# Feeding the second batch beside its own attention, and loading the base by whole parities on GpSimd's queue

## The chip, the cores and the metric

One core of one Trainium2 chip runs the whole kernel. The metric is the device time of one launch in microseconds (us). The engines are called PE (TensorE, matrix products and transposes), DVE (VectorE), ACT (ScalarE), POOL (GpSimd) and SP (SyncE, which only issues transfers here). SP, ACT and POOL each issue DMA transfers in the order of their own instruction queue; a transfer that has to wait for a semaphore makes that queue wait.

## What is computed

Two layers on an input of 2 batches, 128 channels and 64 x 64 positions (L = 4096 tokens of 128 channels per batch). Cut to what matters:

```python
# layer 0: group norm, q/k/v with rotary positions, 4 heads of softmax attention, projection
x = xi + w_proj @ attention(q, k, v) + b_proj
# layer 1, on tokens t of shape (2, 4096, 128)
t = t + softmax(ln(t) @ ln(t).T) @ ln(t)
u = ln(t)
# u convolved along the tokens with 16 spectral filters (plus and minus),
# each result mixed by a 128 x 128 matrix; and three taps of the tokens themselves
t = t + sum_k conv(u, phi_k) @ M_k + sum_i shift(u, i) @ M_u[i]
```

`ln` is a layer norm over the 128 channels. A choice among four branches (by `log_weights + gumbel`) scales the matrices and masks the tail of the sequence.

## The kernel before, in words

The program is written with a tile framework: a tile has a tag and a number of buffers, the framework sets all semaphores, and its scheduler places instructions on the queues near the order of the program; `ordered` and `keep_in_program_order` pin an instruction to that order. Side work is written as Python generators: the main loop calls `next(beside)` at fixed places, and each call emits one step of the side work between the main loop's instructions.

**Stages.** `layer0` runs both batches' first layer. `attend16(0, ...)` is layer 1's attention of batch 0, `attend16(1, ...)` that of batch 1. Then the filter stage: four quarters, one for each batch `b` and parity `ro` of the token blocks, of eight chunks with two steps each, 64 steps in all. Last comes the output.

**Attention (`attend16`, L1241).** The 4096 tokens are eight rows `j` of 512. The 36 pairs (j, i) with i >= j are taken row by row; a turn n handles the scores of pair n (twelve products `y`, L1252), exponentials on ACT (L1261), a 16-bit high part (L1265) and rest (L1266), the direct product `od` of pair n-1, and the transposed product `oa` of pair n-2 (both L1280), whose operand `eT` is made by DMA transposes on SP's queue (L1271). DVE adds up denominators from `eT` (`both`, L1300) and the products (L1292, L1312). A row is finished by `close(j)` (L1314 on), which updates `tok[b]` and calls `closed(j)`: for batch 1 this takes the row's layer norm statistics (`fed`, with the power on POOL, L108), and loads and splits two mixing matrices (L1517 to L1519). `next(beside)` is called four times in a full turn. At the end a loop runs what is left of `beside`.

**Feed (`feed`, L1364).** For a batch it turns the finished tokens into what the filter stage reads. Row `i` of eight: four normalised blocks `un` (L743 through `stats.normed`); for both halves of a transform a product `pf` (L1403), split on ACT and DVE into `uh` (L1375, L1376) and written to DRAM, `rows16[b]`, by four transfers (L1409, L1410); a transpose `uT` (L1422, L1423); the taps, that is a transpose `tT` of the tokens (L1382), three products `ar` (L1387), a sum `oc` (L1390) and its write to DRAM, `base[b]` (L1391). Each of these is a step ended by `yield`. `un`, `uh` and `oc` have two buffers. The taps of row 0 come last, since they need the last row. Feed 0 writes on POOL's queue (`aside`), feed 1 on SP's. Feed 0 runs beside attention 1, with buffers in that stage's pool, and is followed there by the loads of the first step's tables and tokens (`fetch16(0, 4)`, one piece in three calls). Feed 1 runs beside the first quarter of the filter stage, after four empty calls, with buffers in the pool `late`.

**Filter stage.** A step loads 2 MB of tables on SP's queue and 512 KB of tokens (from `rows16[b]`) on POOL's, each for two steps later and into the third of three buffers (`fetch16`, L1202 on; the tokens are L1213, the tables L1222). `convolve16` makes sixteen products `cv` (L1591), ACT and DVE split them into a high part and a rest (L1598, L1599), and `mix16` of the step before adds 48 products `m` (L1607) to an accumulator that is copied out once per chunk to `oh` (L1614). Between four parts of each step, `next(beside)` is called once.

**Back (`back`).** Beside the following quarter, `oh` of a parity is turned (transposes `vt`, L1709, copies L1710) and taken through the inverse transform (`bk`, L1719) in four blocks `p4`; DVE adds the base of the block (`had`, L1721). Outside the last parity a block's base is one transfer of 256 KB on SP's queue into a single buffer (L1703), asked for when the block's turn comes; the first block comes after five empty calls. The last parity has its own loads at the end.

Of the kernel before, what the change touches and what calls it, by code (L numbers as in the profile page):

```python
# [12 lines left out]
F32 = mybir.dt.float32  # L13
# [9 lines left out]
P = 128  # L23
# [22 lines left out]
WC = 4  # L46
# [30 lines left out]
def conv_attn_hybrid(ctx: ExitStack, tc: tile.TileContext, io):  # L77
# [39 lines left out]
    def chain(*parts):  # L117
        for p in parts:
            yield from p
# [638 lines left out]
    def layers(st, layer0, in_halves):  # L758
# [479 lines left out]
        def halves16(n):  # L1238
            return list(zip(tables_in[n % 3], tokens_in[n % 3]))

        def attend16(b, p, beside, closed):  # L1241

            den = p.tile([P, NT, NQ], F32, tag="den", name=f"den{b}")
            oT = p.tile([P, NQ, 512], F32, tag="oT", name=f"oT{b}")
# [113 lines left out]
                        whole = j  # L1358
                    next(beside, None)
            close(whole)  # L1360
            for _ in beside:
                pass

        def feed(b, p, bank, fw, stats=None):  # L1364

            queue = aside if b == 0 else nc.sync


            if stats is None:
# [8 lines left out]
            def taps(i, uT):  # L1378
                oc = p.tile([P, 4, P], F32, tag="oc", name=f"oc{b}_{i}", bufs=2 if in_halves else 1)
                pt = bank(f"tT{b}_{i}").rearrange("p (t c) -> p t c", c=C)  # L1380
                for t in range(4):
                    nc.tensor.transpose(pt[:, t, :], tok[b][:, 4 * i + t, :], ident)  # L1382
                nc.scalar.copy(oc, pt)
                yield
                pa = bank(f"ar{b}_{i}").rearrange("p (t c) -> p t c", c=C)
                for n in range(NU):
                    nc.tensor.matmul(pa, mu[:, n, :], uT[:, 2 - n : 6 - n, :], start=(n == 0), stop=(n == NU - 1))  # L1387
                    if n == 0:
                        yield
                nc.vector.tensor_tensor(oc, pa, oc, ALU.add)  # L1390
                queue.dma_start(base[b][:, 4 * i : 4 * i + 4, :], oc)  # L1391
                yield

            before = first = None
            for i in range(NQ):
                un = p.tile([P, 4, C], F32, tag="un", name=f"un{b}_{i}")
                for t in range(4):
                    stats.normed(un[:, t, :], 4 * i + t)
                yield
                for c in range(2):  # L1400
                    at = BP + 1 + 2 * i
                    pf = bank(f"pf{b}_{i}_{c}").rearrange("p (t c) -> p t c", c=C)
                    nc.tensor.matmul(pf, fw[:, c, :], un, start=True, stop=True)  # L1403
                    if in_halves:
                        uh = p.tile([P, 2, 4, C], F16, tag="uh", name=f"uh{b}_{i}_{c}")
                        uhr = uh.rearrange("w h (p r) d -> w h p r d", r=2)
                        parts(uh, pf)
                        for h in range(2):
                            queue.dma_start(to[:, c, h, 2 * i : 2 * i + 2, :], uhr[:, h, :, 0, :])  # L1409
                            queue.dma_start(to[:, c, h, at : at + 2, :], uhr[:, h, :, 1, :])  # L1410
                    else:
                        uh = p.tile([P, 4, C], F32, tag="uh", name=f"uh{b}_{i}_{c}")
                        uhr = uh.rearrange("w (p r) d -> w p r d", r=2)
                        nc.scalar.copy(uh, pf)
                        queue.dma_start(to[:, c, 2 * i : 2 * i + 2, :], uhr[:, :, 0, :])
                        queue.dma_start(to[:, c, at : at + 2, :], uhr[:, :, 1, :])
                    yield

                uT = p.tile([P, 6, P], F32, tag="uT0" if i == 0 else "uT", name=f"uT{b}_{i}", bufs=1 if i == 0 else 2)
                pt = bank(f"uT{b}_{i}").rearrange("p (t c) -> p t c", c=C)  # L1420
                for t in range(4):
                    nc.tensor.transpose(pt[:, t, :], un[:, t, :], ident)  # L1422
                nc.vector.tensor_tensor(uT[:, 2:, :], pt, mask.unsqueeze(1).to_broadcast([P, 4, P]), ALU.mult)  # L1423
                if i:
                    nc.vector.tensor_copy(uT[:, :2, :], before[:, 4:, :])
                    yield
                    yield from taps(i, uT)
                else:
                    first = uT
                    yield  # L1430
                before = uT
# [25 lines left out]
        with ExitStack() as l1:  # L1457
# [3 lines left out]
            with ExitStack() as part:  # L1461
# [13 lines left out]
                    second_parts(i + 1)  # L1475

                second_parts(0)
                fw = transform(p1)

                def closed(j):  # L1480
                    gate[0] = j + 1
# [15 lines left out]
            if in_halves:  # L1497
                early = pool(middle, "early", side="right")
                tables_early = [early.tile([P, BP, NS, 2 * NK], F16, name=f"tables_e{n}") for n in range(2)]
                tokens_in = [  # L1500
                    [early.tile([P, NS, C], F16, name=f"tokens{turn}_{n}") for n in range(2)] for turn in range(3)
                ]
                tables_in.append(tables_early)
            if in_halves:
                mxr, mxl = mixing
            else:
                mxr, mxl = (x[0].rearrange("p (k s c) -> p k s c", k=NK, s=2) for x in (hiT, loT))
            with ExitStack() as part:
                p = pool(part, "l1_b", 2)
                fed = LayerStats(ffw, tok[1], "f1")  # L1510

                def closed(j):
                    fed.take(range(4 * j, 4 * j + 4))
                    fed.close(range(4 * j, 4 * j + 4))
                    own = slice(2 * j, 2 * j + 2)
                    m = p.tile([P, 2, 2, C], F32, tag="m", name=f"m{j}")
                    aside.dma_start(m, mx[own].rearrange("k p s c -> p k s c"))  # L1517
                    nc.vector.tensor_copy(mxr[:, own], m)
                    nc.vector.tensor_tensor(mxl[:, own], m, mxr[:, own], ALU.subtract)  # L1519

                if in_halves:
                    attend16(1, p1, chain(feed(0, p, bank, fw), spaced(fetch16(0, 4))), closed)
                else:
                    attend(1, p1, feed(0, p, bank, fw), closed)
        psum_a.close()
# [1 line left out]

        pc = pool(st, "ff_psum", space=bass.MemoryType.PSUM)
        pf = pool(st, "ff_x")
        late_pool = pool(right1, "late", 2, side="right")  # L1530

        if in_halves:
            second = px.tile([P, 2, BP, NS, 2 * NK], F16, tag="a", name="tables_a")
# [139 lines left out]
        def back(b, ro, oh, outs, p):  # L1673
# [2 lines left out]
            ohr = oh.rearrange("e (w p c) -> e c p w", c=2, p=BP)  # L1676
            baser = base[b].rearrange("c (q r) j -> c r q j", r=2)
            if not end:
                for _ in range(WC + 1):
                    yield  # L1680
            if ro == 0:
# [14 lines left out]
            def turned(p4):  # L1696

                u = f"{b}_{ro}_{p4}"
                if end:
                    had, v = ends[p4][0], ends[p4][1].rearrange("p (c q) x -> p c q x", c=2)  # L1700
                else:
                    had = p.tile([P, 4, P], F32, tag="had", name=f"had{u}", bufs=1)
                    nc.sync.dma_start(had, baser[:, ro, 4 * p4 : 4 * p4 + 4, :])  # L1703
                    v = p.tile([P, 2, 4, C], F32, tag="v", name=f"v{u}", bufs=1)
                for c in range(2):
                    pt = pc.tile([P, 512], F32, tag="cv", name=f"vt{u}_{c}", bufs=3) if end else one_bank(f"vt{u}_{c}")
# [33 lines left out]

        outs = [None, None]
        late = iter(())
        fw = transform(late_pool)
        beside = chain([None] * WC, feed(1, late_pool, one_bank, fw, fed))
        steps = 0
        for b in range(B):
            for ro in range(2):
# [168 lines left out]
```

## Time and profile before

| what | us |
|---|---|
| median of 3 runs (lowest, highest) | 2737.7 (2715.2, 2753.86) |
| the profiled execution | 2752.7 |
| its span, first to last instruction | 2750.9 |
| PE busy in the span | 2580.7 (94%) |
| ACT busy | 1838.6 (67%) |
| DVE busy | 1671.5 (61%) |
| POOL busy | 437.6 (16%) |
| DMA share of the SP queue (q1), of 16 engines' span | 33.4% |
| DMA share of the POOL queue (q0) | 12.2% |

"Busy" doesn't count the issue of transfers or waiting. An average over the span hides the stages, which have different limits; so the working below reads stretches of 55 us, the waits inside a stage, and the order of issues on a queue. In a line of waits, "A <- B: total, times, longest" says that A's engine sat idle until B was done. In a timeline, the columns are start, length, engine, line and operation, with the idle time before it and what ended it in brackets. The trace records each 32-bit matrix product of PE as two.

### The profile page before, as it was taken

The numbers are of one execution on the slowest core, as the hardware profiler recorded it, in microseconds if no ns is written. First come the engines' busy times: TensorE is split into PE (matmuls) and PEld (weight loads), VectorE is DVE, ScalarE is ACT, GpSimd is POOL, SyncE is SP. The second block draws the span as 40 slices with busy tenths as digits, with TensorE's granted clock in tenths as the row PEclk, the third lists the DMA queues.
The fourth block names the chain that finished last, engine by engine and source line by source line (L and its number), as shares of the span: only waits on it lengthen the run. The fifth ranks groups of instructions, "written<-read, shape, count | busy, mean of one in ns | idle before, by whom it ended". The sixth has DMA issues, their size and how long they took to land.

```text
span 2750.9 us, 32560 instructions
## 1 busy us (share of the span) xinstructions
PE 2580.7 (94%) x11955; PEld 1276.4 (46%) x11955; DVE 1671.5 (61%) x2946; ACT 1838.6 (67%) x2059; POOL 437.6 (16%) x716
## 2 busy tenths in 40 slices
PE   5999999999998999999989996888989999899998
PEld 3555555555544454444444442433444444344444
DVE  5256564246367427888976776655556666566664
ACT  4999999999998897666545563444435554454553
POOL 2022121012122401000333101111111111111110
PEclk9999999999999999999999998999999999999999
DMA  5122220012113514766466955666656666665661
GB/s 145 35 66 66 64 70 20 5 53 66 30 34 98 80 42 83 123 110 105 98 136 124 162 106 132 140 152 154 164 163 175 206 195 156 171 202 176 186 185 59
DMA packets 350827, 311.92 MB, mean 113 GB/s; under 512 B 293296, under 2 KB 302144, under 8 KB 334464
## 3 DMA queue, kind: packets, MB, share of 16 engines
q1 hardware_dynamic: 295920, 231.18, 33.4%
q0 software_dynamic: 53296, 76.13, 12.2%
q10 hardware_dynamic: 1440, 2.43, 0.3%
q8 instruction: 96, 1.57, 0.2%
q14 instruction: 75, 0.61, 0.1%
HBM read 212.53 MB, written 23.33 MB: 86 GB/s over the span
## 4 chain that ended last, share of the span: by engine, by line
PE 63%; DMA 18%; DVE 10%; ACT 6%; issue 2%; SPq 0%; POOL 0%; DVEq 0%; ACTq 0%; POOLq 0%
PE m L1607 17%; PE acc L209 11%; PE s L209 11%; PE cv L1591 5%; DMA rows<-uh 5%; PE od L1280 5%; ACT e L465 5%; PE y L1252 5%; PE oa L1280 4%; DMA had<-base 4%; DMA eT<-pair 2%; DMA tables_b<-tables 2%; DMA tables_a<-tables 2%; DVE x L1599 1%; DVE pair L1266 1%
## 5 line engine op out<-in xcount | busy, mean ns | idle before, releaser
L465 ACT ACTIVATE e<-s 128x1536 f16<-128x1536 f32 (+1 forms) x704 | 938.7, 1425 | 57.0 <-PE s L209 52.3
L1598 ACT CAST x<-cv 128x1024 f16<-128x1024 f32 x512 | 493.6, 1016 | 411.6 <-PE cv L1591 402.5
L1599 DVE TENSOR_TENSOR x<-cv,x 128x1024 f16<-128x1024 f32 x512 | 602.5, 1219 | 267.9 <-ACT x L1598 267.9
L1607 PE MATMUL m<-x,mxr 128*128 128x512 f16 x2048 | 623.4, 381 | 0.0
L209 PE MATMUL acc<-e,v 128*97 128x512 f16 x2048 | 560.1, 381 | 16.3 <-DVE accs L413 13.7
L209 PE MATMUL s<-qs,ks 128*128 128x512 f16 x2048 | 560.5, 381 | 7.3 <-ACT e L465 3.8
L1607 PE MATMUL m<-x,mxl 128*128 128x512 f16 x1024 | 393.2, 384 | 3.2 <-DVE oh L1614 3.2
L209 PEld LDWEIGHTS <-v 128*97 128x97 bf16 x2048 | 255.8, 125 | 230.3 <-issue 29.8
L1261 ACT ACTIVATE ey<-y,nshift 128x512 f32<-128x512 f32 x288 | 196.1, 687 | 189.9 <-PE y L1252 161.7
L1607 PEld LDWEIGHTS <-mxr 128*128 128x128 f16 x2048 | 201.5, 98 | 243.6 <-issue 6.6
L209 PEld LDWEIGHTS <-ks 128*128 128x128 f16 x2048 | 201.2, 99 | 229.4 <-issue 46.9
L1213 POOL DMA_DIRECT2D tokens<-rows x256 | 155.9, 613 | 864.0 <-PE cv L1591 840.6
L1252 PE MATMUL y<-bothT 128*128 128x512 f16 x864 | 204.4, 382 | 3.3 <-ACT ey L1261 2.4
L1266 DVE TENSOR_TENSOR pair<-ey,pair 128x1024 f16<-128x1024 f32 x144 | 175.0, 1219 | 35.4 <-ACT pair L1265 34.8
L1280 PE MATMUL od<-pair,hi 128*128 128x512 f16 x576 | 184.6, 381 | 5.7 <-DVE oT L1292 4.6
L1300 DVE SCALAR_TENSOR_TENSOR both<-eT 128x512 f16<-128x512 f16 x224 | 153.7, 686 | 48.0 <-DMA eT<-pair 43.6
L413 DVE COPY accs<-acc 97x512 f32<-97x512 f32 x64 | 44.2, 690 | 211.0 <-PE acc L209 210.9
L1591 PEld LDWEIGHTS <-tokens 128*128 128x128 f16 x1024 | 101.3, 100 | 148.8 <-issue 50.2
L1607 PEld LDWEIGHTS <-mxl 128*128 128x128 f16 x1024 | 101.4, 99 | 133.7 <-DVE oh L1614 10.6
L1280 PEld LDWEIGHTS <-hi 128*128 128x128 f16 x1024 | 100.8, 98 | 122.3 <-issue 7.0
L1265 ACT CAST pair<-ey 128x1024 f16<-128x1024 f32 x144 | 150.7, 1047 | 6.5 <-DMA eT<-pair 3.3
L1280 PE MATMUL oa<-eT,hi 128*128 128x512 f16 x448 | 142.8, 380 | 0.9 <-DMA eT<-pair 0.9
(223 smaller groups left out, 2298.9 us busy)
## 6 DMA issues: line engine op xcount, KB each, us to landing
tables_a<-tables SPq DMA_DIRECT2D x42, 1024.0 KB
tables_b<-tables SPq DMA_DIRECT2D x42, 1024.0 KB
tables_e<-tables SPq DMA_DIRECT2D x42, 1024.0 KB
tokens<-rows POOLq DMA_DIRECT2D x256, 128.0 KB, 14.3
tab<-in_rot SPq DMA_DIRECT2D x32, 512.0 KB
ks<-term POOLq DMA_DIRECT2D x112, 64.0 KB, 2.2
qs<-term POOLq DMA_DIRECT2D x112, 64.0 KB, 2.0
accs<-back SPq DMA_DIRECT2D x32, 128.0 KB
```

Source lines behind the costliest of these rows:

```text
L209: tc.keep_in_program_order(nc.tensor.matmul(*args, **kw))
L465: nc.scalar.activation(e[:, own, :], ps[:, own, :], AF.Exp, scale=SCORE_SCALE)
L1213: nc.gpsimd.dma_start(ut[64 * copy : 64 * copy + 64], rows16[b].rearrange("h c r w d -> (h c) r w d")[:, row : row + BP, w0 : w0 + NS, :],)
L1252: nc.tensor.matmul(ps[:, q, :], a[0][:, bass.ts(t, P)], c[0][:, bass.ts(i, 512)], start=(n == 0), stop=(n == 2),)
L1261: nc.scalar.activation(e[:, q, :], ps[:, q, :], AF.Exp, bias=nshift16, accum_out=den[:, t, i : i + 1])
L1266: nc.vector.tensor_tensor(pair[:, 1, own], e, pair[:, 0, own], ALU.subtract)
L1280: nc.tensor.matmul(acc, a[0][:, own], pair(m, t), start=(start and t == 0 and n == 0), stop=(stop and t == 3 and n == 2),)
L1300: nc.vector.scalar_tensor_tensor(both, eT[:, 0, :, u, :], 1.0, eT[:, 1, :, u, :], ALU.mult, ALU.add, accum_out=den[:, 4 * i + u, j : j + 1],)
L1591: ordered(nc.tensor.matmul(pu[:, h, :], ut[:, at, :], tt[:, :, at, :], start=True, stop=True))
L1598: nc.scalar.copy(hi, pur)
L1599: nc.vector.tensor_tensor(lo, pur, hi, ALU.subtract)
L1607: nc.tensor.matmul(acc, m, x, start=(s == 0 and i == 0), stop=(s == 1 and i == len(products) - 1))
```

## The change

It has four parts.

1. `feed` of batch 1 moves from the filter stage into attention 1. It gets a `gate`: row `i` is fed only once `closed(i)` has been called, otherwise the call passes without work. It follows feed 0, taking turns (`by_turns`) with the loads of the first step. What has not been done when attention ends goes on beside the filter stage (`drain=False`), with PSUM buffers of that stage (`banked`), and without the four empty calls.
2. Both feeds use POOL's queue, the pool `late` (now opened before attention 1) and one copy of the transform `fw`, loaded after attention 0.
3. A tap has no pause any more between its first and its second product.
4. `back`, except for the last parity, loads the base of a whole parity in one transfer of 1 MB on POOL's queue, before its empty calls; the four blocks read slices of it.

```diff
--- before.py
+++ after.py
@@ -1238,7 +1238,7 @@
         def halves16(n):
             return list(zip(tables_in[n % 3], tokens_in[n % 3]))
 
-        def attend16(b, p, beside, closed):
+        def attend16(b, p, beside, closed, drain=True):
 
             den = p.tile([P, NT, NQ], F32, tag="den", name=f"den{b}")
             oT = p.tile([P, NQ, 512], F32, tag="oT", name=f"oT{b}")
@@ -1358,12 +1358,13 @@
                         whole = j
                     next(beside, None)
             close(whole)
-            for _ in beside:
-                pass
-
-        def feed(b, p, bank, fw, stats=None):
-
-            queue = aside if b == 0 else nc.sync
+            if drain:
+                for _ in beside:
+                    pass
+
+        def feed(b, p, bank, fw, stats=None, gate=None):
+
+            queue = aside
 
 
             if stats is None:
@@ -1385,7 +1386,7 @@
                 pa = bank(f"ar{b}_{i}").rearrange("p (t c) -> p t c", c=C)
                 for n in range(NU):
                     nc.tensor.matmul(pa, mu[:, n, :], uT[:, 2 - n : 6 - n, :], start=(n == 0), stop=(n == NU - 1))
-                    if n == 0:
+                    if n == 0 and not in_halves:
                         yield
                 nc.vector.tensor_tensor(oc, pa, oc, ALU.add)
                 queue.dma_start(base[b][:, 4 * i : 4 * i + 4, :], oc)
@@ -1393,6 +1394,8 @@
 
             before = first = None
             for i in range(NQ):
+                while gate is not None and gate[0] <= i:
+                    yield
                 un = p.tile([P, 4, C], F32, tag="un", name=f"un{b}_{i}")
                 for t in range(4):
                     stats.normed(un[:, t, :], 4 * i + t)
@@ -1475,7 +1478,7 @@
                     second_parts(i + 1)
 
                 second_parts(0)
-                fw = transform(p1)
+                fw = None if in_halves else transform(p1)
 
                 def closed(j):
                     gate[0] = j + 1
@@ -1501,6 +1504,10 @@
                     [early.tile([P, NS, C], F16, name=f"tokens{turn}_{n}") for n in range(2)] for turn in range(3)
                 ]
                 tables_in.append(tables_early)
+                late_pool = pool(right1, "late", 2, side="right")
+                fw = transform(late_pool)
+                banked = [bank]
+                fed_to = [0]
             if in_halves:
                 mxr, mxl = mixing
             else:
@@ -1517,9 +1524,16 @@
                     aside.dma_start(m, mx[own].rearrange("k p s c -> p k s c"))
                     nc.vector.tensor_copy(mxr[:, own], m)
                     nc.vector.tensor_tensor(mxl[:, own], m, mxr[:, own], ALU.subtract)
+                    if in_halves:
+                        fed_to[0] = j + 1
 
                 if in_halves:
-                    attend16(1, p1, chain(feed(0, p, bank, fw), spaced(fetch16(0, 4))), closed)
+                    ahead = spaced(fetch16(0, 4))
+                    feed_1 = feed(1, late_pool, lambda name: banked[0](name), fw, fed, fed_to)
+                    beside = chain(feed(0, late_pool, bank, fw), by_turns(ahead, feed_1))
+                    attend16(1, p1, beside, closed, drain=False)
+                    for _ in ahead:
+                        pass
                 else:
                     attend(1, p1, feed(0, p, bank, fw), closed)
         psum_a.close()
@@ -1527,7 +1541,8 @@
 
         pc = pool(st, "ff_psum", space=bass.MemoryType.PSUM)
         pf = pool(st, "ff_x")
-        late_pool = pool(right1, "late", 2, side="right")
+        if not in_halves:
+            late_pool = pool(right1, "late", 2, side="right")
 
         if in_halves:
             second = px.tile([P, 2, BP, NS, 2 * NK], F16, tag="a", name="tables_a")
@@ -1676,6 +1691,9 @@
             ohr = oh.rearrange("e (w p c) -> e c p w", c=2, p=BP)
             baser = base[b].rearrange("c (q r) j -> c r q j", r=2)
             if not end:
+                if in_halves:
+                    whole = p.tile([P, BP, P], F32, tag="had", name=f"had{b}_{ro}", bufs=1)
+                    aside.dma_start(whole, baser[:, ro])
                 for _ in range(WC + 1):
                     yield
             if ro == 0:
@@ -1699,8 +1717,11 @@
                 if end:
                     had, v = ends[p4][0], ends[p4][1].rearrange("p (c q) x -> p c q x", c=2)
                 else:
-                    had = p.tile([P, 4, P], F32, tag="had", name=f"had{u}", bufs=1)
-                    nc.sync.dma_start(had, baser[:, ro, 4 * p4 : 4 * p4 + 4, :])
+                    if in_halves:
+                        had = whole[:, 4 * p4 : 4 * p4 + 4, :]
+                    else:
+                        had = p.tile([P, 4, P], F32, tag="had", name=f"had{u}", bufs=1)
+                        nc.sync.dma_start(had, baser[:, ro, 4 * p4 : 4 * p4 + 4, :])
                     v = p.tile([P, 2, 4, C], F32, tag="v", name=f"v{u}", bufs=1)
                 for c in range(2):
                     pt = pc.tile([P, 512], F32, tag="cv", name=f"vt{u}_{c}", bufs=3) if end else one_bank(f"vt{u}_{c}")
@@ -1740,8 +1761,11 @@
 
         outs = [None, None]
         late = iter(())
-        fw = transform(late_pool)
-        beside = chain([None] * WC, feed(1, late_pool, one_bank, fw, fed))
+        if in_halves:
+            banked[0] = one_bank
+        else:
+            fw = transform(late_pool)
+            beside = chain([None] * WC, feed(1, late_pool, one_bank, fw, fed))
         steps = 0
         for b in range(B):
             for ro in range(2):
```

## The prediction, made before the changed kernel was run

> **What bounds the kernel now.** I read the table of fixed stretches first, because it shows stage by stage whether TensorE (PE) is full. Columns: stretch, length, busy time and count of PE, PEld, DVE, ACT, POOL, then PE clock, DMA share, GB/s.
>
> ```profile
> 1385.00:1440.00 55.00, 48.20 (x197) 22.56 (x196) 39.70 (x93) 24.42 (x50) 17.65 (x26) 0.94 0.69 136
> 1550.00:1605.00 55.00, 55.00 (x260) 25.49 (x259) 41.98 (x97) 36.65 (x78) 1.76 (x2) 1.00 0.69 127
> 1660.00:1715.00 55.00, 35.18 (x138) 14.74 (x138) 32.26 (x53) 22.71 (x25) 8.18 (x12) 0.83 0.60 135
> 1770.00:1825.00 55.00, 40.12 (x166) 17.72 (x164) 24.38 (x28) 17.83 (x21) 4.87 (x8) 0.89 0.65 148
> 1990.00:2045.00 55.00, 43.74 (x209) 22.38 (x208) 27.67 (x27) 20.74 (x23) 6.08 (x10) 0.88 0.55 174
> 2100.00:2155.00 55.00, 54.79 (x254) 24.67 (x253) 37.65 (x34) 31.32 (x33) 9.73 (x16) 1.00 0.61 203
> ```
>
> PE is full with attention alone (1550) and with the filter stage alone (2100). It has holes where the second batch's feed runs beside the filter stage (1660 to 1990), where the base is fetched (1990), and, smaller, where the first batch's feed runs beside attention (1385). The holes are the gain; work that PE does anyway only changes its place.
>
> To size them I used the timeline of the copies of finished accumulators (L1614), one per chunk; the eighth ends a quarter.
>
> ```profile
> 1994.03 0.59 ACT L1614 COPY oh<-m 128x512 f32<-128x512 f32 x1 [1.09 <-PE m L1607]
> ...
> 2242.53 0.59 ACT L1614 COPY oh<-m 128x512 f32<-128x512 f32 x1 [1.10 <-PE m L1607]
> ```
>
> The first convolution starts at 1658.25, so quarter 1 takes 335.8 us; the others (ends 2242.53, 2488.79, 2726.68) take 248.5, 246.3 and 237.9. Undisturbed chunks lie 27.8 apart (2159.19 to 2214.82 is two), so a bare quarter is 222.6.
>
> Next, who waits in quarter 1 (1657 to 2000), by total:
>
> ```profile
> ACT uh L1375 <- DMA rows<-uh: 60.9, 5, 19.6
> DVE uh L1376 <- ACT uh L1375: 54.0, 14, 18.7
> ...
> PE pf L1403 <- DVE uh L1376: 28.7, 3, 15.6
> ```
>
> ACT cannot refill a `uh` buffer before its write to DRAM is done; DVE waits for ACT, PE for DVE. The page's DMA part and SP's timeline say why the write is late:
>
> ```profile
> tokens<-rows POOLq DMA_DIRECT2D x256, 128.0 KB, 14.3
> ...
> rows<-uh POOLq DMA_DIRECT2D x64, 64.0 KB, 3.0
> ```
>
> ```profile
> 1683.21 10.48 SPq L1410 DMA_DIRECT2D rows<-uh  x1
> ...
> 1805.58 13.73 SPq L1222 DMA_DIRECT2D tables_e<-tables  x2
> ```
>
> The same 64 KB write lands in 3.0 us from POOL's queue in attention; on SP's it stands among 1 MB table loads, its issue alone takes 10 us, and the chain shows such writes at 21 to 37 us.
>
> Last, the chain of waits about 1985 to 2045:
>
> ```profile
> 1985.31 29.47 DMA had<-base
> ...
> 2015.93 23.15 DMA had<-base
> ```
>
> Two base loads in a row hold the end: same queue, one buffer, asked for about three calls before use.
>
> **What the Trainium skill says.** "DMA: Bandwidth & Descriptors", Queues, rings and completion order: each DMA engine consumes a queue's descriptors in ring order and alternates between queues by packets. The trace agrees: 3.0 us on POOL's queue against 21 to 37 behind tables. Same page, Anatomy of one DMA: a semaphore wait is spent on the issuing engine, so what stands behind it on that queue waits too; POOL spends 840.6 us so, in front of token loads. "TensorE: Matmul & The Clock Gate", HAM oscillation: idle gaps make the clock drop; the trace has 0.83, 0.89 and 0.88 in the three stretches with holes. So I cost holes by quarter lengths, which contain the slow clock, not by idle time.
>
> **The change, part by part.**
>
> *Feed's PE work.* Eight rows issue 32 pf and 48 ar records at 0.43 us spacing, 64 transposes at 0.11 and 4 pl: 13.8 + 20.7 + 7.0 + 0.4 = 42 us. Quarter 1 is then 222.6 + 42 + 13 (1658.25 to 1671.40, first convolution before the first mix) + **58 of stall**.
>
> *How much moves.* Attention of batch 1 makes 144 calls on its side work: two, later three or four, per block pair. With one pause fewer in each tap, feed 0 needs 59 and ends at the 16th of 36 pairs. Then table prefetch (24) and feed 1 alternate. Rows close at turns 10, 17, 23, 28, 32, 35 and 37 of 38, so the gate lets rows 0 to 4 and most of row 5 through: 33 of feed 1's 50 steps. Left for the filter stage are row 5's taps, rows 6 and 7, and the end: 2.6 + 5.2 + 5.2 + 3.4 = 16 us of PE. So 26 us of PE work moves: −26 in quarter 1, +26 in attention, nothing in sum.
>
> *Quarter 1.* All 64 row writes, 8 base writes and the ul pair leave SP's queue. On POOL's they come after the step's token loads, whose wait (for PE to release the buffer) ends when that step begins; 14.3 us landing of tokens is the nearest row for a write behind them, and a `uh` buffer is wanted again some 21 us later. I take 4 us of remaining stall (0 to 12). At the start, feed work lands in the fill, where DVE is the chain: 4 × 0.34 for un and 2 × 0.69 for uh, +3; but PE has over 9 us free there, which take 4 of the 16. Quarter 1: 222.6 + 13 + 3 + 16 − 4 + 4 = 255, **−81**.
>
> *Attention of batch 1.* +26 of PE. New stalls: in feed 0's phase (1334 to 1512) PE gaps add up to 13 us over eight rows, most of them pf waiting for un, which stands on DVE behind additions that wait for transposes:
>
> ```profile
> DVE both L1300 <- DMA eT<-pair: 34.6, 13, 7.1
> ...
> PE pf L1403 <- DVE un L743: 10.5, 5, 5.3
> ```
>
> That is 1.6 per row, 9 for 5.6 rows. DVE gets 4.4 us per row (un 4 × 0.34, uh 2 × 0.69, uT 0.98, oc 0.69), 25 in all, and has 13 of 55 free at 1550. A row taken as soon as it closes also waits for its statistics: POOL's power (1.2 us) comes between DVE's last statistic and un. Against that, alternating calls leave more time between un and pf. I take **+10** (−10 to 35: the lower end, since nothing excludes that feed fills gaps now empty, 7 of them after 1512). With the PE work **+36**.
>
> *Quarters 2 to 4.* Transposes and inverse cost PE 96 × 0.11, 11 us per parity. Stall: 248.5 − 222.6 − 11 = 15; 246.3 − 222.6 − 11 = 13; the last has a mix without convolution (24.2 for 27.8), 237.9 − 219 − 11 = 8. Twelve loads of 256 KB leave SP; three of 1 MB go to POOL, asked for at the first call of a quarter, needed at the eighth: 7 × 3.47 = 24 us. The trace has no such load. Lower end: 768 KB of the same 512-byte pieces took 9.2 us in a quiet place (mu_raw), 12 scaled (the skill's formula in Anatomy, 2.0 + bytes/436e3, would make it 4.4; the trace decides). Upper end: 512 KB of tokens lands in about 15, so 1 MB behind them 45. I take 25 to 28, since DMA is only 0.61 busy in this stage: 2 us of stall in each where there was one. In quarter 3 most of the stall isn't the base: its first two chunks (to 2311.69) exceed 55.6 by 13.6, the PE work and 3; 10 us appear after the output writes issued at 2304. Those stay. Savings: 13 + 3 − 2 + 6 = **−20**. Issue time on POOL (74 moved issues at 0.6 to 0.7, three at 1 to 1.5) is covered by its waiting; without that cover it would be 55 us of delay to tokens. The second fw load (256 KB) goes: nothing waited for it.
>
> **Sum.** −81 + 36 − 20 = −65 against the profiled 2752.7: 2688. That execution is 15 above the median of 2737.7. If the 15 are stalls that the change removes anyway, the result stays at 2688; if they lie elsewhere it is 2673. I take two thirds of the way: **2678**, −2.2%.
>
> **Rivals.**
> 1. *Attention pays more.* Transposes, table prefetch and row writes share the DMA engines just there: the stretch 1495 to 1550 has a share of 0.92 and a transpose of 9.6 us. Stalls at 35 instead of 10: 2703 (2698 to 2728). Against it: at 1550, with prefetch running, PE lacked nothing. Chance 0.17.
> 2. *The feed stays late* (scheduling puts it into the filter stage after all), or *the base stays late*. Quarter 1 is then 222.6 + 13 + 42 + 10 = 288, −48, and attention pays nothing: with the base −68, about 2675, so place hardly matters, the queue does. If the base stays late, 20 are lost: 2698. Together 0.10, half each.
> 3. *More is gained*: feed 1 fills idle PE in attention, and output writes meet a less loaded queue: 20 better, 2658. Chance 0.15.
> 4. *Slower: tokens behind the base load.* If 1 MB takes 31 us on POOL's queue, at the rate of tokens, the next step's tokens land at 14 + 31 + 15 = 60 us from the quarter's start; they are needed at three steps, 41.7. 18 of stall in three quarters, and the 20 not saved: 2678 + 54 + 20 = 2752, above the median before. It decides once that load takes over 13 us beyond tokens. For it: tokens already take up to 30.5 us. Against: 38% of DMA time is free here. 0.05.
>
> **Numbers.** The forecast has 0.53, own range 2660 to 2697. Its part below 2683 (2% below the median, about what a measurement of this kernel can tell from no change), some 0.6 of it, and rival 3 are faster, and the late feed of rival 2 about as often as not: 0.32 + 0.15 + 0.03 = 0.50. Slower by over 2% (above 2792) only if rival 4 is worse than priced or unseen: 0.03. The rest, 0.47, lies within. The range from 2645 to 2722 leaves out rival 4 and the tails of 1 and 3, about 0.2.
>
> **What would show it.** Right: SP issues only tables, transposes and outputs after 1310; ACT's wait for row writes under 10 us; quarter 1 at 250 to 262; attention's end 30 to 45 later; DVE's wait for had (37.7) under 8; gaps after the outputs remain. Wrong: od or pf gaps of 5 us in attention (rival 1), convolutions waiting for tokens in a quarter's first four steps (rival 4), or row writes still holding ACT in quarter 1.

## The result, and the profile after

| | median, us | lowest to highest | runs |
|---|---|---|---|
| before | 2736.03 | 2715.2 to 2759.44 | 20 |
| changed | 2717.82 | 2701.15 to 2758.58 | 20 |

The ratio is 0.9938 (95% interval 0.991 to 0.9966): faster, but by 0.6% where 2.2% was forecast. A second set of runs gave 0.9968 (0.9932 to 1.0003), and medians of 2741.49 against 2737.54 before, so that set shows no gain. Ratios leave out executions more than 1.5% above the fastest of their kernel; the first profile of the changed kernel (2752.85 us) and those of queue_deep and pause_pool are such executions, so no stage length is read from them, and the lines here are from a second profile of the changed kernel (after_again, 2712.15 us, span 2710.1).

The stretches of the second profile, with the columns of the prediction's first table; attention of batch 1 ends at 1709, quarter 1 at 1982:

```profile
1385.00:1440.00 55.00, 46.34 (x174) 21.18 (x172) 38.00 (x85) 22.72 (x48) 22.24 (x31) 0.88 0.58 122
1550.00:1605.00 55.00, 53.73 (x248) 25.15 (x247) 40.51 (x88) 34.33 (x73) 11.13 (x15) 1.00 0.78 146
1720.00:1775.00 55.00, 53.28 (x239) 25.15 (x238) 39.68 (x44) 28.07 (x34) 20.89 (x32) 1.00 0.64 205
1815.00:1870.00 55.00, 38.93 (x154) 16.04 (x153) 22.50 (x20) 19.00 (x20) 8.44 (x15) 0.81 0.55 141
1985.00:2040.00 55.00, 55.00 (x303) 31.71 (x302) 37.54 (x36) 26.54 (x30) 7.87 (x13) 1.00 0.59 178
2100.00:2155.00 55.00, 53.80 (x249) 24.13 (x248) 36.99 (x32) 30.05 (x32) 9.77 (x16) 1.00 0.59 200
```

The hole where the base was fetched is closed (1985), and PE is nearly full where the feed now ends beside the filter stage (1720). One new hole stands at 1815 with a clock of 0.81, after the feed is over. The copies that end quarters 1 and 2:

```profile
1982.54 0.58 ACT L1629 COPY oh<-m 128x512 f32<-128x512 f32 x1 [1.09 <-PE m L1622]
...
2216.55 0.58 ACT L1629 COPY oh<-m 128x512 f32<-128x512 f32 x1 [1.09 <-PE m L1622]
```

Stage lengths by such copies, in us, for all kernels below. Attention 1 runs from the last transposes of batch 0's attention to the first convolution.

| kernel | attention 1 | quarters 1 to 4 | ratio to before (95%) |
|---|---|---|---|
| before | 335.8 | 335.8, 248.5, 246.3, 237.9 | |
| after_again | 379.7 | 273.1, 234.0, 240.8, 229.4 | 0.9968 (0.9932 to 1.0003) |
| queue_only | 334.3 | 316.9, 248.8, 233.3, 232.6 | 0.9898 (0.986 to 0.9936) |
| move_only | 381.2 | 248.6, 233.3, 235.4, 239.1 | 0.9848 (0.9801 to 0.9895) |
| base_only | 334.2 | 332.1, 235.8, 244.8, 232.2 | 0.992 (0.9884 to 0.9956) |
| pinned | 382.9 | 250.2, 248.1, 233.5, 229.4 | 0.9936 (0.99 to 0.9973) |
| base_act | 383.0 | 258.6, 256.7, 251.6, 259.6 | 1.0095 (1.0059 to 1.0131) |
| base_sp | 382.1 | 267.7, 232.9, 233.2, 229.4 | 0.9841 (0.9798 to 0.9883) |
| pause | 367.4 | 249.6, 232.8, 234.3, 231.2 | 0.9814 (0.977 to 0.9857) |
| base_runs | 380.8 | 284.8, 239.3, 233.7, 229.4 | 0.9885 (0.981 to 0.9961) |
| queue_deep | | | 0.9876 (0.9824 to 0.9928) |
| pause_sp | 367.7 | 249.6, 232.8, 233.2, 229.4 | 0.9802 (0.9758 to 0.9847) |
| un_ahead | 370.7 | 248.9, 234.4, 242.7, 239.0 | 0.9842 (0.9792 to 0.9893) |
| merged | 379.2 | 282.5, 249.7, 233.2, 236.0 | 0.998 (0.995 to 1.0009) |
| pause_pool | | | 0.9842 (0.9772 to 0.9912) |
| merged_best | 371.9 | 264.5, 232.8, 234.1, 229.7 | 0.9828 (0.9782 to 0.9875) |
| copy_sp | 380.1 | 285.1, 285.1, 279.7, 279.9 | 1.0522 (1.0474 to 1.0571) |
| spread | 378.6 | 253.3, 238.5, 236.3, 231.6 | 0.9917 (0.9882 to 0.9951) |

The stage lengths come from one execution each, the ratios from many; where the two disagree, the ratio is the verdict. Each ratio is to the kernel before in the same set. The sets are the four kernels from after_again to base_only; pinned, base_act, base_sp and pause; base_runs, queue_deep, pause_sp and un_ahead; merged, pause_pool and merged_best; copy_sp and spread.

Who waits in quarter 1 of the changed kernel (1709 to 1983):

```profile
POOL tokens L1213 <- DMA tokens<-rows: 101.1, 32, 6.8
...
PE cv L1606 <- issue: 18.5, 3, 10.0
...
POOL tokens L1213 <- DMA had<-base: 9.9, 1, 9.9
...
ACT uh L1376 <- PE pf L1406: 3.8, 2, 2.0
```

ACT no longer waits for row writes here; it was 60.9 us. Instead POOL waits for earlier token loads. ("issue" means that the profile names no releaser.) Transfers of the whole kernel by issue, with the median time to landing:

```profile
tokens<-rows POOLq DMA_DIRECT2D x256, 128.0 KB, 27.2
...
rows<-uh POOLq DMA_DIRECT2D x128, 64.0 KB, 4.3
...
had<-base POOLq DMA_DIRECT2D x3, 1024.0 KB, 21.7
```

A token load lands 27 us after its issue, not 14. POOL's timeline at the new hole:

```profile
1802.40 1.20 POOL L1696 DMA_DIRECT2D had<-base  x1 [5.82 <-DMA rows<-ul]
1803.60 1.24 POOL L1213 DMA_DIRECT2D tokens<-rows  x2
1808.91 0.61 POOL L1213 DMA_DIRECT2D tokens<-rows  x1 [4.08 <-PE cv L1606]
1814.48 0.61 POOL L1213 DMA_DIRECT2D tokens<-rows  x1 [4.95 <-DMA tokens<-rows]
1818.30 0.61 POOL L1213 DMA_DIRECT2D tokens<-rows  x1 [3.21 <-DMA base<-oc]
1822.14 0.61 POOL L1213 DMA_DIRECT2D tokens<-rows  x1 [3.24 <-DMA tokens<-rows]
1829.53 0.61 POOL L1213 DMA_DIRECT2D tokens<-rows  x1 [6.78 <-DMA tokens<-rows]
1840.02 0.61 POOL L1213 DMA_DIRECT2D tokens<-rows  x1 [9.88 <-DMA had<-base]
```

The first base load is not at the start of quarter 2 (1982), where the program asks for it, but in quarter 1, where the feed has just ended and nothing pins the load. It lands after 37.3 us, and the eighth load after it waits for it. PE's convolutions start again only at 1814, 1829 and 1848, after 18.5 us of waiting together, and chunk 4 takes 47.9 us instead of 27.8. The profile names no releaser for these waits, but the chain from 1795 to 1860 goes through a token load issued right behind the base load, 40 us before it lands:

```profile
1803.60 39.95 DMA tokens<-rows
```

### The profile page after: what moved, and what is told of

Same layout as the page of the kernel before. It is cut to its first block, busy times and chain, and to the rows that moved or that the text cites. A ratio compares the mean times of both kernels' runs of the same rounds, so it can differ in the third digit from the quotient of the medians.

```text
span 2751.0 us, 32520 instructions
## 1 busy us (share of the span) xinstructions
PE 2585.8 (94%) x11955; PEld 1277.3 (46%) x11955; DVE 1671.0 (61%) x2946; ACT 1840.3 (67%) x2059; POOL 492.9 (18%) x792
## 4 chain that ended last, share of the span: by engine, by line
PE 33%; DMA 13%; DVE 6%; issue 5%; ACT 1%; POOL 1%; SPq 0%; DVEq 0%; POOLq 0%; ACTq 0%
PE m L1622 17%; DMA tokens<-rows 10%; PE cv L1606 6%; PE od L1280 3%; PE oa L1280 3%; PE y L1252 3%; DMA eT<-pair 2%; DVE pair L1266 2%; DVE x L1614 1%; DVE both L1300 1%; PE bk L1740 1%; PE pf L1406 1%; ACT ey L1261 1%; PE ar L1388 1%; PE vt L1730 0%
## 5 line engine op out<-in xcount | busy, mean ns | idle before, releaser
L209 PE MATMUL acc<-e,v 128*97 128x512 f16 x2048 | 562.1, 382 | 15.7 <-DVE accs L413 13.1
```

What stands on the lines that cost most here:

```text
L209: tc.keep_in_program_order(nc.tensor.matmul(*args, **kw))
```

## The experiments

**What each part does alone.** Theory A: POOL's queue has no room beside the token loads of the filter stage. Theory B: attention pays more than was reckoned.

> The changed kernel once more, for a second profile. Theory A (GpSimd's queue has no room in the filter stage, so rows and base on it make token loads late): a ratio of 0.99 to 1.00, quarter 1 at 265 to 290 us, quarter 2 at 240 to 265, token loads landing in over 20 us all through. Theory B (attention pays: the feed there costs far more than its PE work): quarters 1 and 2 near 255 and 235 and attention of batch 1 longer by 50 us or more. My prediction's numbers: attention +36, quarters 255, 235, 244, 232.

> The kernel before, with one edit: the second batch's feed, still beside the filter stage, writes on GpSimd's queue. Theory A: the row writes stand among token loads, token loads land later than 14 us, quarter 1 falls from 336 only to 300 to 325, ratio 0.985 to 1.00. Theory B: quarter 1 falls to about 288, as predicted, ratio 0.98 to 0.985.

```diff
-            queue = aside if b == 0 else nc.sync
+            queue = aside
```

> The changed kernel with the base loads as before (256 KB each on SP's queue, asked for late). Theory A, with the base load as the main part of it: token loads land in 14 to 18 us from quarter 2 on, quarter 1 at 255 to 265, quarter 2 back to 245 to 250, ratio 0.98 to 0.99, faster than the changed kernel by 10 us or more. Theory B: as slow as the changed kernel or slower by up to 15 us (base waits return).

 (the changed kernel without its fourth part)

> The kernel before with the base load of a whole parity on GpSimd's queue and nothing else. Theory A: base waits of 38 us go, but token loads land in over 20 us after the load and convolutions wait for them: ratio 0.998 to 1.01. Theory B: about 20 us gained, as predicted: ratio 0.99 to 0.995.

 (the kernel before with the fourth part alone)

Measured, all on one chip: the feed's move without the base, 0.9848; with the base, 0.9968, and the two intervals don't meet. So the fourth part undoes most of what the move earns, though alone it earns 0.8%, as theory B said: theory A's 0.998 to 1.01 for base_only is a miss. There the same loads land in 18.1, 24.2 and 20.8 us and tokens in 26 to 29 us from quarter 2 on, and still convolutions wait for tokens for only 7.3 us in those quarters (and 2.8 without a named releaser). Quarter 1 is 248.6 without the base load and 273.1 with it. In move_only POOL waits for PE again, that is, its loads run ahead of need:

```profile
POOL tokens L1213 <- PE cv L1606: 657.5, 108, 16.3
...
POOL tokens L1213 <- DMA tokens<-rows: 9.1, 4, 3.8
```

I had expected the base waits to return in move_only, with quarter 2 at 245 to 250; it is 233.3. The first block's load goes out at 1789.0 instead of 1985.3, and DVE waits half as long for the base, where it was 37.7 us:

```profile
DVE out L1736 <- DMA had<-base: 18.7, 4, 10.6
```

In the changed kernel theory A holds for quarter 1 and the ratio, but not for quarter 2 (234.0). In part theory B holds too: attention is 44 to 45 us longer, not 36. In queue_only quarter 1 falls to 317, not to the 288 of my second rival. Its row writes land late among tokens (1658 to 1980), and PE waits 17.4 us for `uh`:

```profile
tokens<-rows POOLq DMA_DIRECT2D x68, 128.0 KB, 18.1
rows<-uh POOLq DMA_DIRECT2D x64, 64.0 KB, 15.1
```

**Place or queue of the base load.**

> The changed kernel with the base load held at its place in the program (start of the next quarter) instead of where the scheduler put it (quarter 1, chunk 4, between token loads); only the order on GpSimd's queue differs. Theory A1 (the place is the cause: at that point the queue has no lead): quarter 1 falls from 273 to 250, quarter 2 stays under 240, ratio 0.98 to 0.985. Theory A2 (the queue is the cause wherever the load stands: its share is used up by token loads): the 20 us of stall move into quarter 2, ratio 0.99 to 0.998.

> The same pinned load of a whole parity, on ScalarE's queue. Theory A2: no queue with token loads or tables is in its way, token loads stay at 14 to 22 us, quarters 1 to 4 at 249, 234, 234, 231, ratio 0.978 to 0.984. Theory A1: equal to the pinned load on GpSimd's queue within 0.3%. If the DMA engines as such are the limit, quarter 2 has 10 us or more of stall here too.

> The same pinned load of a whole parity on SP's queue, among the tables, as one load of 1 MB. Theory A2 (the queue with token loads is the tight one): tables take the delay, about 1 MB in 2 MB per step, and have three buffers: stall under 5 us per quarter, ratio 0.98 to 0.987. If lead in any queue is what counts: 5 to 15 us per quarter, ratio 0.987 to 0.995.

```diff
-                    aside.dma_start(whole, baser[:, ro])               # one of the three lines:
+                    ordered(aside.dma_start(whole, baser[:, ro]))      # pinned
+                    ordered(nc.scalar.dma_start(whole, baser[:, ro]))  # base_act
+                    ordered(nc.sync.dma_start(whole, baser[:, ro]))    # base_sp
```

Pinned, quarter 1 recovers (250.2), but quarter 2 takes the loss (248.1), and the ratio is that of the changed kernel:

```profile
DVE out L1742 <- DMA had<-base: 15.5, 1, 15.5
```

So the choice between these two places only decides which quarter pays. On SP's queue the same pinned load costs nothing that the ratio shows: 0.9841, with an interval apart from that of pinned, and DVE never waits for it, so it landed within the 37, 32 and 32 us before its use. SP works further ahead of PE than POOL, though: it issued the first load at 1952.32, 37 us before its use, POOL at 1960.55, 18 us before it was wanted. A load pinned that much earlier on POOL's queue was not run. On ACT's queue it took 50 to 64 us (1953.81 to 2010.64, 2210.80 to 2260.88, 2460.90 to 2524.60, issue to use), and PE stood behind DVE in each quarter:

```profile
PE vt L1730 <- DVE out L1742: 57.9, 3, 25.7
```

My expectation for ACT's queue, the best of the three, was the wrong way round. Stall in quarter 2 here was my sign for DMA engines that are short as such. But they were busy only 0.63, 0.66 and 0.59 of the time while these loads were under way, and 0.70 and 0.78 during base_sp's first two, for which nothing waited: the engines had room that ACT's queue did not get.

Quarter 1 of base_sp needs a second reading. It is 267.7, although no base load is under way before 1952.32 and none is on POOL's queue at all. PE waits 7.6 us for tokens there (1705 to 1973), and POOL as long for its own earlier loads as in the changed kernel:

```profile
POOL tokens L1213 <- DMA tokens<-rows: 122.0, 37, 6.7
```

So late token loads in quarter 1 need no base load. Pinned and pause have such waits too (114.0 and 99.3 us), and PE hardly stops in them; move_only with 9.1 is the exception. What goes with a 1 MB load in the middle of quarter 1 is that the convolutions stop for long: with one it lasts 273.1 to 284.8 us (after_again, base_runs, merged), without one 248.6 to 267.7 in nine profiles (all others with the move but copy_sp). The price of the load there is thus between 5 and 36 us; 24.5 is the distance to move_only.

**Bytes, pieces, or loads in flight.**

> The changed kernel with the base kept in DRAM by parity, so that the same 1 MB load, at the same place on GpSimd's queue, reads runs of 8 KB instead of 2048 pieces of 512 bytes. If the number of pieces is what holds up the token loads behind it: the load lands in 8 to 15 us instead of 21 to 41, quarter 1 at 250 to 255, ratio 0.98 to 0.987. If it is the 1 MB as such: quarter 1 stays at 265 to 285, ratio 0.99 to 0.998.

Cut to the layout; the lines that write and read the base follow it:

```diff
-    base = [dram.tile([C, NI, P], F32, ...) for b in range(B)]
+    base = [dram.tile([C, 2, BP, P], F32, ...) for b in range(B)]
```

> The changed kernel with one token load for both halves of a step (256 KB, 4 KB runs): two loads a step instead of four, same bytes, base load on GpSimd's queue at nearly the same place. In the profile of the changed kernel the eighth load after the base load waits for it. Theory L (the number of loads in flight is the limit, so a slow base load takes a place that tokens need): waits of GpSimd's queue for earlier transfers vanish, quarter 1 at 249 to 258, quarter 2 under 238, ratio 0.978 to 0.987. Theory S (the queue's share of the DMA engines is the limit): quarter 1 stays at 265 to 285, convolutions wait for tokens as before, ratio 0.988 to 0.998.

Cut to the load; the convolution takes its two halves from the one tile:

```diff
-                            ut[64 * copy : 64 * copy + 64],
-                            rows16[b]...[:, row : row + BP, w0 : w0 + NS, :],
+                            tokens_in[n % 3][64 * copy : 64 * copy + 64],
+                            rows16[b]...[:, row : row + BP, w0 : w0 + 2 * NS, :],   # first half only
```

With runs of 8 KB the first load still needs 28 us (1799.58, and a token load released by it at 1827.37), and quarter 1 is 284.8: in this profile the number of pieces is not what stops PE. The three loads land in 27.5, 28.9 and 12.8 us, against 37.3, 20.8 and 21.7 in the changed kernel, and the ratio's interval (0.981 to 0.9961) doesn't exclude a gain. With half as many token loads POOL hardly ever waits for a transfer in front of a token load (1.8 us in quarter 1), only for PE,

```profile
POOL tokens L1213 <- PE cv L1607: 748.0, 54, 28.7
```

and yet PE's convolutions stop (26.9 us in quarter 1), quarter 1 is 282.5 and the ratio 0.998. Theory L, the limit on loads in flight, falls: the eighth-load wait seen above is a symptom.

**Whose room is short.**

> The changed kernel with the second copy of each step's tokens loaded on SP's queue instead of GpSimd's: the same bytes on the DMA engines, but half the tokens (256 KB a step) on the queue that carries the base load, which stays where it was. Theory S (the queue's share is used up by token loads): the base load finds room, quarter 1 at 249 to 258, quarter 2 under 238, ratio 0.978 to 0.987. If the DMA engines as a whole are short of room there: quarter 1 at 265 to 285 as in the changed kernel, ratio 0.988 or more.

```diff
-                        nc.gpsimd.dma_start(
+                        (nc.sync if copy else nc.gpsimd).dma_start(
```

The transfers of POOL's queue (1750 to 2700), base load at the same place:

```profile
tokens<-rows POOLq DMA_DIRECT2D x110, 128.0 KB, 9.9
...
had<-base POOLq DMA_DIRECT2D x3, 1024.0 KB, 17.1
```

With half the tokens gone from it, the queue lands the base in 17.1 us instead of 21 to 37, and no convolution waits for tokens. That is what theory S says of the queue's share. The kernel as a whole is 5% slower, since SP's token loads wait for PE with tables behind them:

```profile
SPq L1213 <- PE cv L1606: 394.8, 86, 7.4
```

```profile
PE cv L1606 <- DMA tables_e<-tables: 37.1, 18, 4.5
```

So the total that I expected is wrong, by a wait on SP's queue that I had not counted. Its landing times don't settle theory S either: quarters of 280 to 285 us leave every queue more time, and base_only, with all the tokens on POOL's queue, landed its first load in 18.1 us.

> The changed kernel with the base of a parity in four loads of 256 KB on GpSimd's queue, held in program order at three to four calls' distance in the next quarter. Theory S: the queue has some room left in each step, so smaller portions pass: quarter 1 at 250, quarters 2 to 4 at 233 to 240, ratio 0.98 to 0.987. If any further byte on that queue is paid by token loads: quarters 2 to 4 at 242 to 250, ratio 0.99 or more.

Its profile is what theory S hoped for (253.3, 238.5, 236.3, 231.6), its ratio, 0.9917 (0.9882 to 0.9951), is not; it can't be told from that of one load (0.9938 and 0.9968). Its runs go from 2690.47 to 2772.87, those of base_sp only from 2680.95 to 2704.47. Why kernels that move the feed and load the base on POOL's queue spread so far stays open.

**What attention pays for.**

> The changed kernel with the base loads of before (as in move_only) and the pause between a tap's first and second product put back. If the missing pause costs (un on DVE has one call less of head start before pf): attention of batch 1 falls from 381 to 372 to 376, PE's waits for un from 17 to 11. If the feed's DVE work as such costs: 379 to 385. What is left of the feed for quarter 1 grows by two or three steps either way.

```diff
-                    if n == 0 and not in_halves:
+                    if n == 0:
```

Attention falls from 381.2 to 367.4. PE's wait for un there (1330 to 1700), of pause and, for comparison, of move_only (1330 to 1710):

```profile
PE pf L1406 <- DVE un L743: 10.7, 9, 1.6
```

```profile
PE pf L1406 <- DVE un L743: 16.7, 8, 5.2
```

The longest wait is 1.6 instead of 5.2 us. The third part of the change, the pause taken out, costs 14 us of attention between these two profiles, with the same number of PE's instructions (1480 and 1479). Only 6.0 of them are waits for un; another 4.9 are PE's busy time, which falls from 344.3 to 339.4 at a granted clock of 0.99 instead of 0.97. The other profiles agree: attention takes 378.6 to 383.0 us in nine without the pause and 367.4 to 371.9 in four with it. By the ratio it isn't shown: base_sp has 0.9841 and pause_sp, which differs from it by the pause alone, 0.9802, with overlapping intervals.

> As pause (base loads as before, pause put back), and each row's un made one row's taps earlier where the gate allows it. If PE's waits in attention are un's missing head start: waits for un fall from 11 us to under 4, attention from 367 to 357 to 362, ratio 0.975 to 0.981. If DVE's load as such: attention stays at 364 to 372.

A still earlier un brought nothing: attention is 370.7. PE's waits for un fall to 6.9 us, not to under 4, and 7.6 us of waits for uT take their place. This says nothing of the whole kernel, since base waits differ.

> The changed kernel with only the pause in the tap put back. If pause and base load are separate causes: attention 367 as with pause, quarters as in the changed kernel (265 to 285, then 234 to 245), ratio 0.984 to 0.993. If later feed steps move the base load out of the tight place: quarter 1 at 255 or less, ratio 0.978 to 0.983.

0.9842 (0.9772 to 0.9912): the interval touches that of the changed kernel (from 0.991), so a gain with the base still on POOL's queue is likely and not shown.

**Two more.**

> The kernel with only the queue changed (queue_only), and four buffers instead of two for each row write of the second batch's feed; the order of every queue is the same. If late landing behind token loads times two buffers is what held its quarter 1 at 317 us: 285 to 295, ratio 0.98 to 0.985. If the waits of GpSimd's queue for earlier transfers hold it: 310 to 320.

0.9876 against 0.9898 for queue_only: no difference that the intervals show. In its one profile PE no longer waits for uh (17.4 us in queue_only) but for tokens (13.1 us, and 10.8 without a named cause): there the deeper buffer moved the wait from writes to loads on the same queue.

> The pause in the tap put back, and the base load of a whole parity early on SP's queue. Base waits are gone on SP's queue and attention has its head start: attention 367, quarters 250, 233, 233, 229, ratio 0.977 to 0.983, equal to the pause alone within 0.3%, since that one has under 5 us of base waits.

> As pause_sp (pause put back, base of a parity early on SP's queue), with one token load for both halves of a step. Theory L: nothing to gain in the profile of a good run (its quarters are full already), but no run falls behind: ratio 0.977 to 0.981, lowest to highest within 15 us. Theory S: equal to pause_sp, 0.977 to 0.984.

Both are as fast as pause, within their intervals. pause_sp, the feed's move with the pause kept and the base of a parity early on SP's queue, has the lowest ratio here: 0.9802 (0.9758 to 0.9847), 2679.69 us in the median, against 2738.66 before in the same set. Its interval meets those of pause, base_sp, move_only and merged_best.

## Why the prediction was wrong

The direction was right, the size was not: 0.6% against 2.2%, outside the own range of the likeliest case. The step that failed is the term of the fourth part in *Quarters 2 to 4*: a gain of 20 us credited to it, at a price of 2 us of stall a quarter. Without that part the forecast would have been 2698 (its second rival, base late), and move_only measured 2697.0. With it the ratio rose from 0.9848 to 0.9968 in one set, 33 us, where a fall of 20 us was forecast (against the first set's 0.9938 it is 25). That 2698 fits so well is partly luck, as the steps show, each in single profiles:

- *Feed's PE work, nothing in sum*: right. Attention without the new stalls would be 335.8 + 26 = 362; with the pause kept it is 367. *How much moves* was right too: 24 of feed 1's 32 pf records and 24 of its 48 ar records are made in attention 1, as reckoned.
- *Quarter 1 at 255*: right without the base load (248.6, against 222.6 + 13 + 16 − 4 = 247.6 with no stall at all), wrong in the change (273.1). Row writes on POOL's queue hold neither ACT nor PE, as reckoned.
- *Attention +36*: measured +44. The term mis-sized is the stall, 18 instead of 10. I took the missing pause for fewer calls only; keeping it makes attention 14 us shorter, 6.0 of them through shorter waits for un. The prediction's line for DVE's additions (34.6) counts beyond feed 0's phase; from 1334 to 1512 it is 21.6.
- *Quarters 2 to 4, −20*: the step that failed, in its gain and in its price. Alone, part four brings just the gain: 712.8 against 732.7 us. But the move alone already brings −25 (707.8). With the feed gone earlier, the first base load goes out earlier and DVE waits half as long for the base. With both, the three quarters are 704.2, so part four added only 3.6. And the load's price, which I set to 2 us of stall a quarter "since DMA is only 0.61 busy in this stage", came to 24.5 us in quarter 1 against move_only. The load landed in 37.3 us there, not in 25 to 28. DMA engines that are busy 0.61 of the time on average, and POOL's long waits for PE, did not tell how much one queue can take. A token load (128 KB, four in a step of 13.9 us) landed 14.3 us after its issue, so about four of them were under way at any time. I had read that row as 512 KB landing in about 15 us, a queue with nothing left over, and still added 1 MB a quarter to it.
- *What the load uses up* (an account that fits, not shown): tokens are asked for two steps ahead, 27.8 us and 1 MB, the size of one base load. In quarter 1 with the feed moved most of that lead is gone: tokens land after 27.6 us in the changed kernel (median), and after 27.4 us in pause, where PE doesn't stop yet. A base load put in front of them stops it. In base_only tokens landed after 13.8 us before its first load came, and PE hardly stopped. No run changed the lead alone.
- *Asked for at the first call of a quarter*: wrong for the first load, which the scheduler placed in quarter 1, in the queue's tightest stretch. Pinned shows that the other place moved the loss to the next quarter.
- *Rival 4* had the mechanism, tokens behind the base load, but at three places and with 0.05. The profile shows it at one, and not in a quarter's first four steps, the sign that was named, but during chunks 3 and 4 of quarter 1. *Rival 2*'s "place hardly matters, the queue does" was wrong: 317 instead of 288.
- *What would show it*: ACT's wait for row writes (3.9 us) and DVE's for `had` (none) came under their limits; quarter 1 missed its 250 to 262, and attention ended 51 us later, not 30 to 45 (7 of the 51 lie before it).
- *From profile to median*: the changed kernel's profile is 41 us below the one before (2752.7 to 2712.15), of which −63 + 44 − 29 are the stages and +7 lie before attention 1, in work that the change doesn't touch. The medians differ by 18. I carried most of a profile's stall over to the median. For move_only too the profiles differ by 64 us and the medians by 41; there the −25 in quarters 2 to 4, which I had not counted for the move alone, made up for it.

Shown: moving the base load from SP's to POOL's queue turns most of the gain back, wherever of the two places it stands and with half as many token loads; and the missing pause makes attention longer in every profile. Supported, not shown: that this queue had no room left for it, and that the number of pieces doesn't matter. Open: how much of SP's advantage is its earlier request, why quarter 1 of base_sp and merged_best is long without a base load in it, and why the changed kernel's runs spread so far.

## What to carry to other kernels

Before a transfer is moved to a queue, compare how long that queue's regular loads take to land with how often they are due and how far ahead they are asked for; where landing takes as long as the lead, an added load can stop the consumer, however idle the issuing engine and the DMA engines are on average. Two edits that remove the same wait are worth it once: cost the second against the kernel with the first. A wait that grows after a change need not come from it: compare with kernels that lack the suspected part. A pause in hand-interleaved side work may be the head start of the next step, and a transfer that must come late needs to be pinned in this framework, not just written late.

## What the runs showed of the hardware that I had not expected

The same 1 MB load took 18 to 37 us on POOL's queue (base_only, after_again, pinned), at most 37, 32 and 32 on SP's among the tables, and 50 to 64 on ACT's queue, on which nothing else was issued meanwhile: the emptiest queue was the slowest while the others were busy. Runs of 8 KB instead of 512-byte pieces brought no clear gain on POOL's queue (27.5, 28.9 and 12.8 us, against 37.3, 20.8 and 21.7).
